# Scores and exp by halves of the queries, in the last two blocks of a cross-attention loop

## The chip, the cores and the metric

The kernel runs on one core of one Trainium2 chip. The metric is the device time in microseconds (us) of one execution. The engines are TensorE (PE in the profile; its weight loads are PEld), VectorE (DVE), ScalarE (ACT), GpSimd (POOL) and SyncE (SP), which issues most transfers.

## The reference

One block of a Perceiver: cross-attention of 512 tokens to a context of 8192, then linear attention, then a quantized feed-forward layer. The change touches the cross-attention only:

```python
x = x + xattn(layernorm(x), ctx, ctx, Wq, bq, Wk, bk, Wv, bv, Wo, bo)
# xattn, 16 heads of 32, x (1, 512, 512), ctx (1, 8192, 512), all f32:
q = split_heads(query @ Wq + bq)
k = split_heads(key @ Wk + bk)
v = split_heads(value @ Wv + bv)
scores = einsum('bhqd,bhkd->bhqk', q, k) / sqrt(d)
weights = softmax(scores, axis=-1)
z = einsum('bhqk,bhkd->bhqd', weights, v)
return merge_heads(z) @ Wo + bo
```

## The kernel before

The context is cut into 16 blocks of 512 positions. A block has 16 units: four groups `g` of four heads (32 rows each, so a group fills 128 partitions) times four chunks `k` of 128 context positions. The loop (line 837) runs over the 256 units in order of block, group, chunk. For a unit:

- `weights` (line 773) makes the scores: 8 matmuls, one for each head `j` and each half `h` of the 128 positions, that each write 64 partitions by 512 queries. Each shows as two instructions, so a unit has 16 (line 788). They go to `sc`, a PSUM tile of 128 x 4 x 512 f32: for each partition four rows of 512, one a head. The pool `ps_s` has one such tile. One ACT instruction then takes the exp of all 2048 columns into `ex` (line 797), a tile in SBUF with four buffers.
- Next on PE come steps from a queue of projections for later blocks (`ahead`; matmuls of line 388 into `pm` or `pk`, evicted by lines 405, 478, 481, 491), and the weighted sums of the *previous* unit (`weighted_sums`, line 733, into `av`). In the last block the weighted sums come first, then one step, and at times row sums of the exps (`sums`, line 751, into `dn`).
- DVE adds `ex` to a running sum `acc` (line 806), from which the softmax denominators come, and the finished `av` to `Z` (line 745).

How many projection steps a unit takes is planned by cost and due time: up to block 13 each block's work makes the next block's keys and values. In block 14 (total - 2) there is less, because part of the last block's keys (22 units of cost) is kept for the last block itself. Block 15 (total - 1) runs those, one step a unit, until they are used up.

All these instructions are kept in the order in which the program issues them on each engine; the framework adds the waits between engines.

After the loop follow the output projection (line 898), linear attention (lines 936 to 1123; `feat` of lines 1051 and 1073 are its features, with exps of 128 x 1024 at line 1029) and the feed-forward layer. The kernel has a second, exact variant (`exact`), taken only if a denominator is out of bounds; the change leaves it as it is.

Of the kernel before, what the change touches and what calls it, by code (L numbers as in the profile page):

```python
# [8 lines left out]
F32 = mybir.dt.float32  # L9
BF16 = mybir.dt.bfloat16  # L10
AF = mybir.ActivationFunctionType
# [5 lines left out]
P = 128  # L17
# [9 lines left out]
def network(  # L27
# [24 lines left out]
    nc = tc.nc  # L52
    S, E = x.shape
    L = ctxT.shape[1]
    FF = W1T.shape[1]
    H, D = 16, 32
# [3 lines left out]
    HG = P // D  # L60
# [3 lines left out]
    SCALE = 1.0 / float(D) ** 0.5  # L64
# [12 lines left out]
    def in_order(i):  # L77

        return tc.keep_in_program_order(i)
# [6 lines left out]
    for i in range(7):  # L86
        n = 1 << i
# [190 lines left out]
    ap4 = ctx.enter_context(tc.tile_pool(name="ap4", bufs=4))  # L278
    ps_m = ctx.enter_context(tc.tile_pool(name="ps_m", bufs=2, space=PSUM))

    with ExitStack() as actx:
        aw = actx.enter_context(tc.tile_pool(name="aw", bufs=1))

        qT = aw.tile([P, NE, S], F32, name="qT")
# [11 lines left out]
        bias = aw.tile([P, NE], F32, name="bias")  # L296
# [4 lines left out]
        ct, kT, vt, tt = {}, {}, {}, {}  # L301
# [4 lines left out]
        total = first + NB  # L306
# [418 lines left out]
        ps_s = sctx.enter_context(tc.tile_pool(name="ps_s", bufs=1, space=PSUM))  # L725
# [36 lines left out]
        def biased(g):  # L762
# [5 lines left out]
            else:  # L768
                in_order(nc.vector.tensor_scalar(
                    Z[:, g, :], Z[:, g, :], bv_sb[:, g : g + 1], None, ALU.add  # L770
                ))

        def weights(b, g, k):

            assert ("k", b, g, k // 2) in made
            sc = ps_s.tile([P, HG, S], F32, name="sc")
            if exact:
                for j in range(HG):
                    for h in range(2):
                        in_order(nc.tensor.matmul(  # L780
                            sc[ts(h, P // 2), j, :], lhsT=ones_h[ds(j * D, 3), ts(h, P // 2)],
                            rhs=mrow[ds(j * D, 3), g, :], start=True, stop=False,
                        ))

            for j in range(HG):
                rows = ts(j, D)
                for h in range(2):
                    in_order(nc.tensor.matmul(  # L788
                        sc[ts(h, P // 2), j, :],
                        lhsT=kT[b][rows, g, ds(k * P + h * P // 2, P // 2)],  # L790
                        rhs=qT[rows, g, :], start=not exact, stop=True,
                    ))
            ex = ap4.tile([P, HG, S], F32, name="ex")
            if exact:
                in_order(nc.scalar.activation(ex, sc, AF.Exp, scale=SCALE))
            else:
                in_order(nc.scalar.activation(  # L797
                    ex, sc, AF.Exp, bias=bias[:, g : g + 1], scale=SCALE
                ))
            return ex  # L800
# [35 lines left out]

        for i, u in enumerate(units):
            ex = weights(*u)
            if i >= last_block:
                b, g, k = u  # L840
# [470 lines left out]
    for q in range(NF // 4):  # L1311
# [14 lines left out]
        for i in range(4):  # L1326
# [8 lines left out]
            if f < 2 or i % 2 == 1:  # L1335
                k = f if f < 2 else f // 2 + 1
# [33 lines left out]
    for i in range(len(chunks) + 1):  # L1370
        if i < len(chunks):
            f, n = chunks[i]
# [4 lines left out]
        f, n = chunks[i - 1]  # L1377
# [18 lines left out]
@with_exitstack  # L1396
def perceiver_block(ctx: ExitStack, tc: tile.TileContext, **args):
    nc = tc.nc
    fate = ctx.enter_context(tc.tile_pool(name="fate", bufs=1))
    wrong = fate.tile([1, 1], mybir.dt.int32, name="wrong")  # L1400
    network(tc, False, wrong, **args)
    again = nc.values_load(wrong, min_val=0, max_val=1)
    with tc.If(again > 0):
        network(tc, True, None, **args)
# [50 lines left out]
```

## Time and profile before

| what | value |
|---|---|
| median of 3 runs | 1117.11 us (1117.04 to 1119.11) |
| the profiled execution | 1118.67 us, span 1116.9 us |
| granted TensorE clock, mean | 0.995 |
| block 14 (848.7 to 902.2): PE, DVE, ACT busy | 51.34, 43.67, 32.54 us of 53.50 |
| block 15 (902.2 to 955.8): PE, DVE, ACT busy | 49.10, 43.88, 34.52 us of 53.60 |
| granted clock in both | 1.00 |

Times in the profile are counted from the start of the span. A line of the timeline has the start, the duration, engine, source line, operation, output and inputs, shapes and count; the brackets give how long the engine was idle before it and whose end released it. Several instructions of one kind in a row are merged, and the duration is then that of the whole row. Matmuls are pipelined and their ends are modelled, so a start is surer than an end. A line of a group has, behind the bar, busy us, mean ns of one, and idle us before them. A line of the waits has total us, times, and the longest. A line of a stretch has its length, then busy us (and instructions) of PE, PEld, DVE, ACT and POOL, then the granted clock and what the transfers took.

### The profile page before, as it was taken

How to read it: one execution, taken by the hardware profiler on the slowest of the kernel's cores; microseconds unless marked ns; L12 is line 12 of the kernel's file. 1: busy time of each engine (PE TensorE's matmuls, PEld its weight loads, DVE VectorE, ACT ScalarE, POOL GpSimd, SP SyncE). 2: the span in 40 equal slices, each digit the busy share in tenths (PEclk: the TensorE clock that was granted, in tenths of full speed). 3: DMA queues.
4: the chain of work that ended last, by engine and by line, in shares of the span. 5: the costliest groups of instructions: out<-in, count | busy, mean ns of one | idle time of the engine just before them, and what ended most of it. 6: DMA issues, size and time to landing. Idle time of an engine off the chain costs nothing.

```text
span 1116.9 us, 31051 instructions
## 1 busy us (share of the span) xinstructions
PE 1089.1 (98%) x14331; PEld 409.7 (37%) x14336; DVE 932.2 (83%) x863; ACT 633.7 (57%) x425; POOL 177.8 (16%) x90
## 2 busy tenths in 40 slices
PE   8999999999999999999999999999999999999896
PEld 5433333333333333333333333333332321344342
DVE  3688999999888888888888888888888888756796
ACT  2155555566666666666665555555555566346253
POOL 3520303011403030403030303030300000023000
PEclk9999999999999999999999999999999999999999
DMA  7121213110302121212010101010110021130001
GB/s 264 38 79 40 96 40 96 58 59 30 95 31 68 50 76 30 75 51 68 30 58 2 40 2 40 2 39 2 40 39 2 2 77 39 38 151 2 1 1 41
DMA packets 24778, 55.56 MB, mean 50 GB/s; under 512 B 1984, under 2 KB 2496, under 8 KB 24384
## 3 DMA queue, kind: packets, MB, share of 16 engines
q1 hardware_dynamic: 24352, 52.97, 14.3%
q8 instruction: 114, 1.87, 0.7%
q10 hardware_dynamic: 288, 0.52, 0.1%
q14 instruction: 24, 0.20, 0.1%
HBM read 48.25 MB, written 5.24 MB: 48 GB/s over the span
## 4 chain that ended last, share of the span: by engine, by line
PE 88%; ACT 5%; DVE 5%; issue 1%; DMA 1%; SPq 0%; DVEq 0%; ACTq 0%
PE pm L388 35%; PE sc L788 24%; PE av L733 18%; ACT ex L797 4%; PE po L898 2%; PE pq L1007 2%; PE pq L136 1%; DVE unchanged L143 1%; PE pv L936 1%; PE pys L1356 1%; DVE de L1122 1%; ACT er L1029 1%; PE att L1112 1%; DMA ct<-in_ctxT 1%; DVE tops L631 0%
## 5 line engine op out<-in xcount | busy, mean ns | idle before, releaser
L797 ACT ACTIVATE ex<-sc,bias 128x2048 f32<-128x2048 f32 x256 | 504.3, 1970 | 358.4 <-PE sc L788 358.4
L806 DVE TENSOR_TENSOR acc<-acc,ex 128x2048 f32<-128x2048 f32 x248 | 584.8, 2358 | 73.2 <-ACT ex L797 72.9
L788 PE MATMUL sc<-qT,kT 32*64 32x512 f32 x4096 | 285.2, 613 | 6.9 <-ACT ex L797 6.7
L733 PE MATMUL av<-ex,vt 128*32 128x512 f32 x2048 | 266.9, 593 | 0.0
L383 POOL TENSOR_TENSOR tt<-ct 128x512 f32<-128x512 f32 x32 | 62.4, 1950 | 573.4 <-DMA ct<-in_ctxT 519.8
L788 PEld LDWEIGHTS sc<-qT,kT 32*64 32x64 f32 x4096 | 59.7, 129 | 221.8 <-ACT ex L797 198.0
L388 PE MATMUL pm<-w,tt 128*32 128x256 f32 x2048 | 127.0, 382 | 0.0
L388 PE MATMUL pm<-tt,w 128*32 128x256 f32 x1920 | 118.0, 382 | 0.0
L388 PE MATMUL pm<-w,ct 128*32 128x256 f32 x1536 | 96.5, 383 | 0.0
L478 DVE TENSOR_TENSOR vt<-vt,pm 128x512 f32<-128x512 f32 x112 | 75.3, 684 | 25.1 <-PE pm L388 24.1
L388 PEld LDWEIGHTS pm<-w,tt 128*32 128x32 f32 x2048 | 59.7, 109 | 86.0 <-issue 51.9
L388 PE MATMUL pm<-ct,w 128*32 128x256 f32 x1440 | 90.1, 383 | 1.2 <-DMA ct<-in_ctxT 1.2
L733 PEld LDWEIGHTS av<-ex,vt 128*32 128x32 f32 x2048 | 65.3, 110 | 55.5 <-issue 14.0
L383 POOL TENSOR_TENSOR tt<-ct,tt 128x512 f32<-128x512 f32 x32 | 85.3, 2666 | 1.3
L388 PEld LDWEIGHTS pm<-tt,w 128*32 128x32 f32 x1920 | 56.5, 109 | 77.6 <-issue 46.2
L388 PEld LDWEIGHTS pm<-w,ct 128*32 128x32 f32 x1536 | 43.3, 109 | 73.8 <-issue 47.0
L388 PEld LDWEIGHTS pm<-ct,w 128*32 128x32 f32 x1440 | 41.2, 109 | 67.2 <-issue 44.1
L478 DVE TENSOR_TENSOR kT<-kT,pm 128x512 f32<-128x512 f32 x60 | 40.8, 680 | 27.6 <-PE pm L388 27.0
L481 DVE SCALAR_TENSOR_TENSOR kT<-pm,bk_sb,kT 128x256 f32<-128x256 f32 x90 | 39.0, 474 | 2.9 <-PE pm L388 1.0
L745 DVE TENSOR_TENSOR Z<-Z,av 128x512 f32<-128x512 f32 x60 | 40.6, 677 | 0.0
L1029 ACT ACTIVATE er<-feat 128x1024 f32<-128x1024 f32 x32 | 30.2, 1029 | 9.7 <-PE feat L1051 7.4
L1033 DVE SCALAR_TENSOR_TENSOR f<-er 128x1024 f32<-128x1024 f32 x16 | 19.9, 1248 | 13.6 <-ACT er L1029 13.6
(181 smaller groups left out, 585.7 us busy)
## 6 DMA issues: line engine op xcount, KB each, us to landing
ct<-in_ctxT SPq DMA_DIRECT2D x15, 1024.0 KB, 5.3
wraw<-in_W1T SPq DMA_DIRECT2D x16, 512.0 KB, 3.8
wraw<-in_W2T SPq DMA_DIRECT2D x16, 512.0 KB, 3.8
wd<-wquant SPq DMA_DIRECT2D x16, 256.0 KB, 2.4
w_q<-wd SPq DMA_DIRECT2D x2, 2048.0 KB, 10.6
w<-in_w_qkv SPq DMA_DIRECT2D x3, 1024.0 KB, 5.1
w<-in_Wk SPq DMA_DIRECT2D x2, 512.0 KB, 6.5
ct<-in_ctxT SPq DMA_DIRECT2D x2, 512.0 KB, 7.5
```

The source lines that it names most:

```text
L383: in_order(nc.gpsimd.tensor_tensor(tt[b][:, i], x, y, ALU.subtract))
L388: in_order(nc.tensor.matmul(ps[ts(j, D)], lhsT=lhsT[:, ts(j, D)], rhs=rhs, start=start, stop=stop))
L478: in_order(nc.vector.tensor_tensor(dst, src, ps, ALU.add))
L481: in_order(nc.vector.scalar_tensor_tensor(dst[:, m, :], ps[:, m, :], bk_sb[:, 2 * i + m : 2 * i + m + 1], src[:, m, :], ALU.add, ALU.add,))
L733: in_order(nc.tensor.matmul(av[g][ts(j, D), :], lhsT=vt[b][:, k, ds(g * P + j * D, D)], rhs=ex[:, j, :], start=(k == 0), stop=(k == NC - 1),))
L745: in_order(nc.vector.tensor_tensor(Z[:, g, :], Z[:, g, :], ps, ALU.add))
L788: in_order(nc.tensor.matmul(sc[ts(h, P // 2), j, :], lhsT=kT[b][rows, g, ds(k * P + h * P // 2, P // 2)], rhs=qT[rows, g, :], start=not ex ...
L797: in_order(nc.scalar.activation(ex, sc, AF.Exp, bias=bias[:, g : g + 1], scale=SCALE))
L806: in_order(nc.vector.tensor_tensor(acc[:, g], acc[:, g], ex, ALU.add))
L898: in_order(nc.tensor.matmul(po, lhsT=lhsT[:, c, ts(t, P)], rhs=w[:, c, :], start=(c == 0), stop=(c == NE - 1),))
L1007: in_order(nc.tensor.matmul(ps, lhsT=wt[:, c, ts(g, P)], rhs=ynT[:, c, :], start=(c == 0), stop=(c == NE - 1),))
L1029: in_order(nc.scalar.activation(er[-1][:, d].rearrange("p a n -> p (a n)"), ps[h], function))
```

## The change

In blocks 14 and 15, `weights` makes the scores of queries 0 to 255 for all heads, takes their exp, then makes the scores of queries 256 to 511 and takes theirs. The matmuls are twice as many with 256 columns each, and so are the exps with 1024 columns (four runs of 256). The tile `sc` is allocated once, in the first of these units, and kept for all 32 of them. The order of everything else stays.

```diff
+        halved = {}
+
         def weights(b, g, k):
 
             assert ("k", b, g, k // 2) in made
+            if not exact and b >= total - 2:
+
+
+                if "sc" not in halved:
+                    halved["sc"] = ps_s.tile([P, HG, S], F32, name="sc")
+                sc = halved["sc"]
+                ex = ap4.tile([P, HG, S], F32, name="ex")
+                for q in range(2):
+                    n = ts(q, S // 2)
+                    for j in range(HG):
+                        rows = ts(j, D)
+                        for h in range(2):
+                            in_order(nc.tensor.matmul(
+                                sc[ts(h, P // 2), j, n],
+                                lhsT=kT[b][rows, g, ds(k * P + h * P // 2, P // 2)],
+                                rhs=qT[rows, g, n], start=True, stop=True,
+                            ))
+                    in_order(nc.scalar.activation(
+                        ex[:, :, n], sc[:, :, n], AF.Exp, bias=bias[:, g : g + 1], scale=SCALE
+                    ))
+                return ex
             sc = ps_s.tile([P, HG, S], F32, name="sc")
```

## The prediction

> **What bounds the kernel now.** I read the page first (busy shares, the chain that ended last), then the groups of instructions by shape, then the timeline of the last two blocks, 848.73 to 955.77 us, and who waited there.
>
> ```profile
> PE 1089.1 (98%) x14331; PEld 409.7 (37%) x14336; DVE 932.2 (83%) x863; ACT 633.7 (57%) x425; POOL 177.8 (16%) x90
> ...
> PE 88%; ACT 5%; DVE 5%; issue 1%; DMA 1%; SPq 0%; DVEq 0%; ACTq 0%
> ```
>
> TensorE (PE) carries the chain. Its busy time is modelled, so I take the spacing of starts instead, in one unit of the last block (timeline; start, duration):
>
> ```profile
> 905.46 0.24 PEld L788 LDWEIGHTS sc<-qT,kT 32*64 32x64 f32 x16 [1.18 <-ACT ex L797]
> 905.46 1.12 PE L788 MATMUL sc<-qT,kT 32*64 32x512 f32 x16 [0.28 <-ACT ex L797]
> ...
> 906.51 1.07 PE L733 MATMUL av<-ex,vt 128*32 128x512 f32 x8
> 906.68 1.97 ACT L797 ACTIVATE ex<-sc,bias 128x2048 f32<-128x2048 f32 x1 [1.27 <-PE sc L788]
> ...
> 907.39 1.04 PE L388 MATMUL pk<-ct,w 128*32 128x512 f32 x8
> ...
> 908.70 0.69 PE L788 MATMUL sc<-qT,kT 32*64 32x512 f32 x8 [0.27 <-ACT ex L797]
> ```
>
> A unit is scores (16 matmul instructions, 1.05 us to the next start), then weighted sums and projections, while ScalarE (ACT) does the exp. The exp starts 1.22 after the scores, takes 1.97, and the next scores start 0.04 later: 3.24 in all. The rest of PE's work would have been done sooner. How much sooner, the weight loads say: before scores that don't wait they are idle for 0.84, before those that do for 1.18, so the wait is 0.34.
>
> ```profile
> 879.14 0.23 PEld L788 LDWEIGHTS sc<-qT,kT 32*64 32x64 f32 x16 [0.84 <-ACT ex L797]
> ```
>
> The waits of 848.7 to 955.8:
>
> ```profile
> PEld sc L788 <- ACT ex L797: 34.6, 32, 2.0
> ...
> PE sc L788 <- ACT ex L797: 6.4, 20, 1.1
> ...
> PE dn L751 <- ACT ex L797: 0.3, 1, 0.3
> ```
>
> So 21 of the 32 units wait for an exp: 18 for 0.34, two for 0.40 and one, at 942.22, for 1.20 (2.04 less 0.84). That is 6.1 + 0.8 + 1.2 = 8.1 us, all that there is to win here. The other 11 are bound by PE's work alone (3.33 to 3.76 each).
>
> **What the change does to a unit.** It issues the same columns in twice the instructions: scores of queries 0 to 255 for all four heads (S0), their exp (E0), scores of 256 to 511 (S1), their exp (E1). Everything turns on one question: may PE write S1 while ACT still reads E0's half, and the next S0 while ACT reads E1's? Both halves lie in the same four 512-column rows of `sc`, one row a head; E0 reads all four rows and each S1 matmul writes one of them. Nothing in this trace shows it: every PSUM tile of the kernel before is written whole before it is read. The nearest row is an early eviction by halves (timeline):
>
> ```profile
> 12.65 1.93 PE L388 MATMUL pm<-ct,w 128*32 128x256 f32 x32
> ...
> 14.74 0.48 DVE L481 SCALAR_TENSOR_TENSOR kT<-pm,bk_sb,kT 128x256 f32<-128x256 f32 x1 [1.02 <-issue]
> ```
>
> These 32 matmuls fill columns 0 to 255 of one 512-column row first and 256 to 511 with the last 16. The VectorE (DVE) addition reads only the first half, ready at about 13.7; DVE was idle from 13.72, yet it starts at 14.74, behind the end of all 32 (14.58). The profile names no releaser, so this is a strong hint, not proof, that the program orders accesses by whole rows. I take "held": S1 waits for E0, and the next S0 for E1. The other bound, "free", is priced below.
>
> The Trainium skill speaks against the change here: PSUM — Partial Sum Buffer, section "PSUM bank collisions raise a hardware error", says that TensorE must not write a 2 KiB bank of PSUM, in the same 32 partitions, while ScalarE reads it, even at disjoint columns, and that the program's semaphores have to keep them apart. By that rule a row of 512 f32 is one such bank and only "held" can run, at the sum below; without it "free" would stay open, at 1109 us. No run here shows a collision.
>
> **The cost of a held unit.** Rows for the half exp and for short scores:
>
> ```profile
> L797 ACT ACTIVATE ex<-sc,bias 128x2048 f32<-128x2048 f32 x256 | 504.3, 1970 | 358.4 <-PE sc L788 358.4
> ...
> L1029 ACT ACTIVATE er<-feat 128x1024 f32<-128x1024 f32 x32 | 30.2, 1029 | 9.7 <-PE feat L1051 7.4 <-PE feat L1073 2.3
> L236 ACT ACTIVATE wquant<-wraw,neg_magic 128x1024 bf16<-128x1024 f32 x16 | 18.2, 1136 | 0.0
> ...
> 987.04 1.21 PE L1051 MATMUL feat<-proj_sb,kT 32*64 32x128 f32 x64
> 988.17 3.27 PE L1007 MATMUL pq<-ynT,w 128*128 128x512 f32 x7
> 988.28 2.85 ACT L1029 ACTIVATE er<-feat 128x1024 f32<-128x1024 f32 x3 [0.55 <-PE feat L1051]
> ```
>
> - Half exp: 1.03 (an exp of 128x1024 without a bias column, half of them strided just like this one) to 1.14 (with a bias column, out of SBUF). Between L797 and the 0.69 of a 128x512 activation with bias (L1117) a straight line gives 1.115; I take that. It also makes 2.23 of ACT time a unit in place of 1.97, which is hidden: ACT is idle for 40 of these 107 us.
> - Half scores: 64 instructions of 128 columns pass in 1.13 (987.04 to 988.17), 16 of 512 in 1.05: the same columns, so 16 of 256 cost 0.52 to 0.565. I take 0.52. The doubled weight loads (0.13 each, overlapping) cost nothing extra in L1051's row; if they showed, 0.565 prices them.
> - From the last scores' pace to the exp: 1.22 - 1.05 = 0.17 at 512 columns, 0.11 at 128 (988.28 - 988.17). I take 0.14.
>
> S0's start to S1's start: 0.52 + 0.14 + 1.115 + 0.045 = 1.82. S1 then runs 0.52 and the other work follows as before. So PE's unit is its old work plus 1.82 + 0.52 - 1.05 = 1.29: E0 has no work behind which to hide, because weighted sums and projections are queued behind S1 on PE. E1 is hidden: 0.14 + 1.115 + 0.045 = 1.30 after S1, beside 1.85 of sums and projections. The old waits for the exp vanish. One unit (938.98, with no projection left) has only about 0.97 there and stays bound by ACT, at 2 x 1.82 = 3.64 instead of 3.33 (3.24 - 1.20 + 1.29).
>
> Sum over the 32 units: 32 x 1.29 = 41.3, less 8.1 of old waits, plus 0.3: 33.5. Five evictions by ACT (four L405 of 0.68, one L491) end about 0.2 after the next S0 is ready to be read, so they delay E0: +1.0. DVE loses nothing: it is busy 87.6 of 107.1 and its units get longer. No transfer is late: the last weights of this stretch are issued by 939 and first read at 972. Total +34.5: the span goes from 1116.9 to 1151.4, the profiled execution from 1118.67 to 1153.2; the median of the runs lies 1.56 below that execution, so 1117.11 becomes 1151.6.
>
> The Trainium skill's ScalarE: Activation LUTs, "What ACT_TABLE_LOAD costs", gives 280 ns + 0.833 ns an element with a bias column, that is 1.133 for a half; the sum by it, an estimate, would be 0.6 us more than by my 1.115.
>
> **Rivals.**
> 1. Free (faster). If the program lets PE write one half of a row while ACT reads the other, exps and scores overlap, and PE never waits: the 8.1 us come back, less about 0.2 where the unit without projection is bound by two exps: 1109.2. It decides if S1 starts before E0 ends. For it: ACT and PE each have room, and DVE just fits (35.2 busy in the 40.0 us from 902.2 to 942.2, which would shrink to 35.7). Against: the eviction at 14.74. Chance 0.05.
> 2. Held, and PE's clock drops (much slower). PE would be idle for a third of each unit. Two stretches point either way (PE busy, then clock):
>
> ```profile
> 1037.00:1048.00 11.00, 8.98 (x47) 2.70 (x50) 6.70 (x5) 4.46 (x5) 0.00 (x0) 0.85 0.00 0
> ...
> 1090.00:1100.00 10.00, 6.64 (x29) 2.52 (x29) 8.37 (x24) 4.80 (x6) 0.00 (x0) 1.00 0.00 1
> ```
>
> At 0.85 the 2.9 us of PE's work in a unit grow by 0.51, 16 us in all: 1168. The gaps here are short (1.3) and come every 4 us, so I give 0.05.
> 3. It changes nothing: the halves run, but each unit's PE work hides E0 as well. That needs sums or projections ahead of S1, and the code issues them after it: 1117. Chance 0.01.
>
> **How the numbers follow.** Held at full clock has 0.89. Its own bounds: half exp 1.03 to 1.14 gives -2.7 to +0.8 (32 units, once each on PE's path), the pace up to 0.565 in both halves +2.9, the latency 0.11 to 0.17 plus or minus 1.0, the delayed E0 -1.0 to +1.0. Together some 1147 to 1157; I widen by 1 for terms that I have not seen: 1146 to 1158, about 0.82 of the chance. A measurement of this kernel can tell 0.2% (2.2 us): slower 0.94 (held, with either clock), same 0.01, faster 0.05.
>
> **What would show it.** Right: 64 half exps near 1.115; in each unit PE idle for about 1.2 before S1, released by the half exp; S1 starting 0.04 after E0 ends; 71 us for block 14 and 70 for block 15, in place of 53.5 each; nothing moved after the loop. Wrong: S1 rows that start during E0 (free), a clock under 1.00 in the loop's end (rival 2), or a half exp whose time is not half of the columns.

## The result, and the profile after

The changed kernel takes 1159.8 us (median of 4 runs, 1159.4 to 1160.5) against 1118.0 for the kernel before beside it: a ratio of 1.0371, 95% interval 1.0358 to 1.0385. That is 41.8 us slower, where 34.5 were forecast: the direction was right and S1 is held as forecast, but the size was too small, and the time lies 1.8 us above the range. The profiled execution took 1159.36, its span 1157.4.

The groups of shapes in the stretch of the last two blocks (848 to 1000 us):

```profile
L795 ACT ACTIVATE ex<-sc,bias 128x1024 f32<-128x1024 f32 x64 | 71.3, 1113 | 70.6 <-PE sc L790 70.6
...
L790 PE MATMUL sc<-qT,kT 32*64 32x256 f32 x1024 | 44.1, 399 | 41.3 <-ACT ex L795 41.3
```

The 64 half exps take 1.113 us each, and PE is idle for 41.3 us before scores, waiting for one (6.4 before the change, in these 32 units). One unit on the timeline, with the next:

```profile
864.40 0.69 PE L790 MATMUL sc<-qT,kT 32*64 32x256 f32 x16
865.20 1.11 ACT L795 ACTIVATE ex<-sc,bias 128x1024 f32<-128x1024 f32 x1 [2.22 <-PE sc L790]
...
866.37 0.69 PE L790 MATMUL sc<-qT,kT 32*64 32x256 f32 x16 [1.27 <-ACT ex L795]
...
866.99 1.06 PE L388 MATMUL pk<-ct,w 128*32 128x512 f32 x8
867.16 1.11 ACT L795 ACTIVATE ex<-sc,bias 128x1024 f32<-128x1024 f32 x1 [0.85 <-PE sc L790]
...
868.84 0.69 PE L790 MATMUL sc<-qT,kT 32*64 32x256 f32 x16
```

S1 starts 0.06 after the end of E0 (865.20 + 1.11): it is held. From S0 to S1 it is 1.97, forecast 1.82. From S1 to the next work it is 0.62, forecast 0.52. Behind that come sums and projections as before, and E1 is hidden beside them. PE's clock is 1.00 through the whole stretch (first numbers after the length: busy us of PE, PEld, DVE, ACT):

```profile
849.36:924.00 74.64, 54.26 (x936) 19.65 (x936) 44.01 (x29) 36.69 (x34) 0.00 (x0) 1.00 0.05 16
924.00:996.00 72.00, 51.11 (x776) 14.30 (x768) 43.84 (x23) 37.70 (x36) 0.00 (x0) 1.00 0.09 30
```

From the first scores of block 14 to the last row sums (997.92) it is 148.56 us, against 107.04 before: 41.5 more. The remainder cancels in part: 0.6 more ahead of block 14 and 1.65 less after the loop, in one execution of each; neither was studied.

### The profile page after: what moved, and what is told of

Same layout as the page of the kernel before. It is cut to its first block, busy times and chain, and to the rows that moved or that the text cites. A ratio compares the mean times of both kernels' runs of the same rounds, so it can differ in the third digit from the quotient of the medians.

```text
span 1157.4 us, 32114 instructions
## 1 busy us (share of the span) xinstructions
PE 1095.7 (95%) x14848; PEld 417.7 (36%) x14848; DVE 932.5 (81%) x863; ACT 642.1 (55%) x457; POOL 176.5 (15%) x90
## 4 chain that ended last, share of the span: by engine, by line
PE 89%; DVE 4%; ACT 4%; issue 1%; DMA 1%; SPq 0%; ACTq 0%; DVEq 0%
PE pm L388 35%; PE sc L811 20%; PE av L733 19%; PE sc L790 4%; ACT ex L795 3%; PE pq L1030 2%; PE po L921 2%; PE pk L388 1%; PE pq L136 1%; DVE unchanged L143 1%; PE pv L959 1%; PE pys L1379 1%; DVE de L1145 1%; ACT er L1052 1%; PE dn L751 1%
## 5 line engine op out<-in xcount | busy, mean ns | idle before, releaser
L820 ACT ACTIVATE ex<-sc,bias 128x2048 f32<-128x2048 f32 x224 | 441.2, 1970 | 318.5 <-PE sc L811 318.5
L811 PE MATMUL sc<-qT,kT 32*64 32x512 f32 x3584 | 249.5, 613 | 0.5 <-ACT ex L820 0.3
L383 POOL TENSOR_TENSOR tt<-ct 128x512 f32<-128x512 f32 x32 | 57.2, 1789 | 574.8 <-DMA ct<-in_ctxT 520.4
L811 PEld LDWEIGHTS sc<-qT,kT 32*64 32x64 f32 x3584 | 52.1, 129 | 187.2 <-ACT ex L820 163.4
L795 ACT ACTIVATE ex<-sc,bias 128x1024 f32<-128x1024 f32 x64 | 71.3, 1113 | 70.6 <-PE sc L790 70.6
L388 PEld LDWEIGHTS pm<-w,tt 128*32 128x32 f32 x2048 | 59.7, 109 | 83.5 <-issue 49.3
L383 POOL TENSOR_TENSOR tt<-ct,tt 128x512 f32<-128x512 f32 x32 | 89.2, 2786 | 1.3
L790 PE MATMUL sc<-qT,kT 32*64 32x256 f32 x1024 | 44.1, 399 | 41.3 <-ACT ex L795 41.3
L790 PEld LDWEIGHTS sc<-qT,kT 32*64 32x64 f32 x1024 | 15.0, 129 | 82.7 <-ACT ex L795 71.8
```

The lines of the kernel that those rows point to most:

```text
L383: in_order(nc.gpsimd.tensor_tensor(tt[b][:, i], x, y, ALU.subtract))
L388: in_order(nc.tensor.matmul(ps[ts(j, D)], lhsT=lhsT[:, ts(j, D)], rhs=rhs, start=start, stop=stop))
L790: in_order(nc.tensor.matmul(sc[ts(h, P // 2), j, n], lhsT=kT[b][rows, g, ds(k * P + h * P // 2, P // 2)], rhs=qT[rows, g, n], start=True, ...
L795: in_order(nc.scalar.activation(ex[:, :, n], sc[:, :, n], AF.Exp, bias=bias[:, g : g + 1], scale=SCALE))
L811: in_order(nc.tensor.matmul(sc[ts(h, P // 2), j, :], lhsT=kT[b][rows, g, ds(k * P + h * P // 2, P // 2)], rhs=qT[rows, g, :], start=not ex ...
L820: in_order(nc.scalar.activation(ex, sc, AF.Exp, bias=bias[:, g : g + 1], scale=SCALE))
```

## The experiments

My theory: S1 is *held* until E0 ends, and since no other work is queued ahead of S1, PE stands still. Most of the loss is that wait (PE idles for 41.3 in place of 6.4 us, by its modelled ends), and the forecast was short because a short row of scores costs more than its columns. The rivals: the doubled number of instructions costs time in itself; the clock drops; and, on why it is held, rows of the tile or the tile as a whole.

**1. What do 256-column scores cost by themselves?** All 32 matmul instructions of a unit in one go, one exp:

```diff
                 for q in range(2):
                     n = ts(q, S // 2)
                     for j in range(HG):
...
-                    in_order(nc.scalar.activation(
-                        ex[:, :, n], sc[:, :, n], AF.Exp, bias=bias[:, g : g + 1], scale=SCALE
-                    ))
+                in_order(nc.scalar.activation(
+                    ex, sc, AF.Exp, bias=bias[:, g : g + 1], scale=SCALE
+                ))
```

> The scores in 256-column halves as in the change, all 32 matmul instructions in one go, then one exp of 2048 columns as before. Measures the price of the short matmuls without any wait between them. Account 'per burst' (a row of scores costs its columns, 0.43 for each 256, plus a fixed 0.19 to whatever follows and 0.37 to the exp, however many instructions it has): scores to next work stays at 1.05, scores to exp at 1.22, time as before, 1118 us within 1. Account 'per instruction' (the 0.62 that 16 instructions of 256 columns took in the changed kernel is 39 ns for each of them): 32 take 1.24, so 0.19 more in every unit, 32 x 0.19 = 6: 1124 us. The prediction's own 0.52 for 16 (columns alone): 1.05, as before, but then the 0.62 has no reason.

Measured: 1119.1 against 1119.2, ratio 0.9995 (0.9983 to 1.0007): no difference. Timeline of this kernel:

```profile
849.03 1.12 PE L790 MATMUL sc<-qT,kT 32*64 32x256 f32 x32
...
850.08 1.93 PE L388 MATMUL pm<-w,ct 128*32 128x256 f32 x32
850.26 1.97 ACT L795 ACTIVATE ex<-sc,bias 128x2048 f32<-128x2048 f32 x1 [1.37 <-PE sc L790]
```

32 short instructions take 1.05 to the next work and 1.23 to the exp, just like 16 long ones. So twice the instructions are free, and 16 short ones, at 0.62, are not half of 1.05. Two points give the account: 0.43 for the columns of a half, and 0.19 once for each row of scores, however long.

**2. Does that account hold at a quarter?**

```diff
-                for q in range(2):
-                    n = ts(q, S // 2)
+                for q in range(4):
+                    n = ts(q, S // 4)
```

> Four quarters of 128 queries in place of two halves. Account 'per burst' (0.21 for the columns of a quarter, 0.37 to the exp, 0.69 for an exp of 512 columns as in the row of line 568, 0.045 back): 1.32 from quarter to quarter, three times, then 0.21 + 0.19: 4.35 in place of 1.05, 3.30 more in each unit, 32 x 3.30 - 8.1 = 97: 1215 us. By the prediction's numbers (columns alone, 0.26 a quarter, 0.14 to the exp): 1.13 from quarter to quarter, 2.61 more in each unit, 32 x 2.61 - 8.1 = 75: 1193 us.

Measured: 1285.6 (a single run), 166 more than before, where neither account gave more than 97. The first unit, at a clock of 1.00, is what the account "per burst" says (timeline):

```profile
851.09 0.47 PE L790 MATMUL sc<-qT,kT 32*64 32x128 f32 x16
...
852.41 0.48 PE L790 MATMUL sc<-qT,kT 32*64 32x128 f32 x16 [0.85 <-ACT ex L795]
...
855.06 0.48 PE L790 MATMUL sc<-qT,kT 32*64 32x128 f32 x16 [0.84 <-ACT ex L795]
...
855.47 3.08 PE L388 MATMUL pm<-w,ct 128*32 128x256 f32 x32
```

It is 1.32 from quarter to quarter, and 0.41 from the last quarter to the next work (0.21 + 0.19; columns alone would be 0.26). Then the clock falls, and with it goes the sum (stretches; the clock is the number behind the five busy times):

```profile
865.00:880.00 15.00, 11.12 (x136) 3.10 (x128) 4.58 (x2) 4.19 (x7) 0.00 (x0) 0.61 0.00 0
880.00:910.00 30.00, 21.26 (x328) 7.76 (x335) 9.85 (x5) 11.19 (x17) 0.00 (x0) 0.67 0.01 2
```

So the total decides nothing here, the spacing at full clock does. And the second rival of the prediction is a real mechanism: it did not act in the profiled run of the change, but in the one run of the next step in the same direction it did.

**3. Is the loss the time beside E0?** The previous unit's weighted sums are put right behind E0's issue, ahead of S1 (the loop's own calls of them, further down, become `between()`):

```diff
+                    if q == 0:
+                        between()
                 return ex
...
-            ex = weights(*u)
+            before, adds = [], []
+
+            def between():
+                while late:
+                    before.append(late[0][-1])
+                    adds.append(weighted_sums(*late.pop(0)))
+
+            ex = weights(*u, between)
...
```

> The change, with the weighted sums of the previous unit put between the two halves on TensorE, right behind the issue of the first exp, so that 0.88 of work lies beside the first exp. Theory (the loss is TensorE's idle time beside the first exp, since no work is queued ahead of the second scores): the wait before the second scores falls by 0.88 or so, and a unit is then bound by ScalarE's chain of two held halves, 2 x 1.96 = 3.92, where 2.9 to 3.3 was TensorE's work; 4.4 in the three units with row sums. Block 14 about 63, block 15 about 64, together 127 in place of 107: 1138 us (1135 to 1142). Rival (the loss is in the twice as many instructions themselves, not in the wait): nothing comes back, 1159.

Measured: 1140.8 against 1119.2, ratio 1.0188 (1.0167 to 1.0210): 21.6 slower, so about half of the loss is back, within the expected range. Timeline:

```profile
857.38 0.69 PE L790 MATMUL sc<-qT,kT 32*64 32x256 f32 x16 [0.28 <-ACT ex L795]
...
859.34 0.69 PE L790 MATMUL sc<-qT,kT 32*64 32x256 f32 x16 [0.28 <-ACT ex L795]
...
859.96 1.06 PE L733 MATMUL av<-ex,vt 128*32 128x512 f32 x8
...
861.30 0.69 PE L790 MATMUL sc<-qT,kT 32*64 32x256 f32 x16 [0.28 <-ACT ex L795]
```

PE's idle time before S1 fell from 1.27 to 0.28, and scores now start every 1.96: the chain of two held halves sets the pace, 3.92 for a unit where a whole one took 3.24. Instructions are as many as in the change, so their number is not the cause.

**4. Why is it held: rows?** The halves by heads, in rows of their own, in the same kept tile:

```diff
                 for q in range(2):
-                    n = ts(q, S // 2)
-                    for j in range(HG):
+                    two = ts(q, HG // 2)
+                    for j in range(2 * q, 2 * q + 2):
...
-                        ex[:, :, n], sc[:, :, n], AF.Exp, bias=bias[:, g : g + 1], scale=SCALE
+                        ex[:, two, :], sc[:, two, :], AF.Exp, bias=bias[:, g : g + 1], scale=SCALE
```

(the matmuls write `sc[..., j, :]` from `qT[rows, g, :]`, all 512 queries).

> The same split into two scores and two exps in the last two blocks, but by heads: scores and exp of heads 0 and 1, then of 2 and 3, all 512 queries, in the same tile that is kept. The order of the score matmuls is then that of the kernel before. Theory 'rows' (in the change the second scores wait for the first exp because both halves lie in the same four 512-column rows of the scores' tile): the two halves now lie in different rows, so nothing is held; TensorE never waits for an exp in these units, the first exp starts before the end of all scores, and up to the 8.1 us of old waits come back: 1110 us (1109 to 1113). Theory 'tile' (the wait comes from writing a tile that ScalarE is reading, wherever): the second scores are held as well, 8 matmul instructions on half of the array take 0.85, so start to start 0.85 + 0.37 + 1.11 + 0.05 = 2.38, a unit grows by 2.38, and 32 x 2.38 - 8.1 = 68: 1186 us.

Measured: 1225.9, ratio 1.0962 (1.0936 to 1.0989). Held, although no matmul of S1 writes a row that E0 reads (timeline, and one stretch):

```profile
869.48 1.09 PE L790 MATMUL sc<-qT,kT 32*64 32x512 f32 x8
870.63 1.11 ACT L795 ACTIVATE ex<-sc,bias 128x1024 f32<-128x1024 f32 x1 [3.76 <-PE sc L790]
...
871.80 1.09 PE L790 MATMUL sc<-qT,kT 32*64 32x512 f32 x8 [1.24 <-ACT ex L795]
...
872.82 1.07 PE L388 MATMUL pk<-ct,w 128*32 128x512 f32 x8
```

```profile
970.00:1000.00 30.00, 25.03 (x144) 4.85 (x143) 14.00 (x8) 10.71 (x10) 0.00 (x0) 0.73 0.00 1
```

S1 starts 0.06 after the end of E0 (870.63 + 1.11). The theory "rows" falls. S0 to S1 is 2.32, expected 2.38 by "tile"; the excess over 1186 comes with a clock of 0.73 to 0.89 in these stretches.

**5. Or the tile?** The same by heads, in two tiles of two rows each:

```diff
-                if "sc" not in halved:
-                    halved["sc"] = ps_s.tile([P, HG, S], F32, name="sc")
-                sc = halved["sc"]
+                if not halved:
+                    sctx.close()
+                    ps_h = sctx.enter_context(tc.tile_pool(name="ps_h", bufs=1, space=PSUM))
+                    for q in range(2):
+                        halved[q] = ps_h.tile([P, HG // 2, S], F32, name=f"sc{q}")
...
```

(the tiles come from a pool opened anew; matmuls and exps use `halved[q]`).

> By heads as in the run by heads before it, which was held although its halves lay in different rows, but with the scores of heads 0 and 1 and those of heads 2 and 3 in two tiles of their own (two rows each), kept for the 32 units. Same instructions, same order. Theory 'tile' (the program waits by whole tiles: a matmul that writes a tile waits for the last instruction that reads it, wherever in the tile): now nothing is held inside a unit, scores run as one row of 1.05, the first exp starts before the second scores end, TensorE never waits for an exp and its clock stays at 1.00. Up to 8.1 us less than before: 1111 us against 1119 (1110 to 1115). Rival (the wait is not the tile's but comes with two exps and two scores on the two engines, for instance because the second scores have to follow the first exp in whatever order is kept between them): 1226 as by heads.

Measured: 1117.3 against 1118.8, ratio 0.9985 (0.9976 to 0.9994). The wait inside the unit is gone, 108 us against the run by heads, by nothing but the two tiles (timeline):

```profile
904.10 1.11 PE L792 MATMUL sc<-qT,kT 32*64 32x512 f32 x16
...
905.26 2.12 ACT L797 ACTIVATE ex<-sc,bias 128x1024 f32<-128x1024 f32 x2 [1.21 <-PE sc L792]
...
907.00 1.51 PE L792 MATMUL sc<-qT,kT 32*64 32x512 f32 x16
...
907.43 0.21 PEld L792 LDWEIGHTS sc<-qT,kT 32*64 32x64 f32 x8 [0.22 <-ACT ex L797]
...
910.30 1.11 PE L792 MATMUL sc<-qT,kT 32*64 32x512 f32 x16
```

So in one tile the second scores wait because the program orders these accesses by whole tiles. But I expected 1111, and that was wrong. The first exp starts 1.16 after the scores, not at half time: two heads are finished hardly sooner than all four (1.22), as if all of them ran side by side on the array (in number 4 two heads alone took 1.15). Both exps then end at 907.38, after 907.00, where PE is ready for the next scores; the second eight of those wait until 907.43, and run alone. A pair of units takes 6.20 in place of 6.48, and only part of the old wait comes back.

**6. Two tiles in all 256 units** (the condition without `b >= total - 2`).

> Two tiles by heads in all 256 units. In the first 14 blocks TensorE's work alone is longer than the chain through the exp (only about a quarter of a microsecond of wait in all of the page's idle time of the scores' matmuls outside the last two blocks), so theory 'tile' gives the same time as with two tiles in the last two blocks, 1111 (1109 to 1115); ScalarE has 0.26 us more in each unit, which is hidden behind its 1.4 of idle time. Rival: evictions by ScalarE and the exps get into each other's way there, or the hold is back: slower than the former by more than 3 us.

Measured: 1116.1 against 1118.8, ratio 0.9978 (0.9968 to 0.9988): the fastest version here, by 2.7 us. It is not told apart from number 5, whose interval overlaps; the level of 1111 failed for the same reason.

**7. The second exp alone.** Scores whole, as in the kernel before, then two half exps (the cut is against number 1):

```diff
-                in_order(nc.scalar.activation(
-                    ex, sc, AF.Exp, bias=bias[:, g : g + 1], scale=SCALE
-                ))
+                for q in range(2):
+                    n = ts(q, S // 2)
+                    in_order(nc.scalar.activation(
+                        ex[:, :, n], sc[:, :, n], AF.Exp, bias=bias[:, g : g + 1], scale=SCALE
+                    ))
```

> Scores whole as before (16 matmul instructions of 512 columns), then two exps of 256 queries each, one behind the other, in the last two blocks. Measures what the second exp alone costs. From the rows: scores to exp 1.22, two exps of 1.113 that overlap by about 0.1, 0.045 back: 3.39 for the chain in place of 3.24. Units that waited take 0.15 more, those of 3.33 take 0.06 more: about 18 x 0.15 + 8 x 0.06 = 3.2 us over the kernel before. If the exps do not overlap: 3.49, about 6 us.

Measured: 1122.7 against 1118.8, ratio 1.0040 (1.0027 to 1.0053), 3.9 us where 3.2 were expected. Waiting units go from 3.24 to 3.40 (907.34 to 910.73 in its timeline, 3.39): two exps in a row cost 2.12.

**8. The change in block 15 alone** (the condition with `total - 1`).

> The change in the last block only. By the sum with the sizes that the changed kernel showed (1.96 + 0.62 - 1.05 = 1.53 for each unit, less the old waits of that block, 5.4, plus 0.35 for the unit without a projection): 16 x 1.53 - 5.4 + 0.35 = 19.4 over the kernel before, and the clock at 1.00. If the loss came from a drop of the clock or from something that builds up over the two blocks, it would be far from half of the 41.

Measured: 1141.0 (2 runs), ratio 1.0197 (1.0179 to 1.0216), 20 to 24 us where 19.4 were expected. That is about half of the 41, so nothing builds up over the two blocks. In the profiled execution (1140.25) block 15, from its first scores (904.14) to the last row sums (979.01), takes 21.3 more than before (902.22 to 955.77). Of these, 1.7 lie in one place: from the S1 at 960.73 to the next scores at 964.89 it is 4.16, where the same step of the changed kernel (981.33 to 983.80) takes 2.47. The row sums in it took 1.90 in place of 1.06, at a clock of 0.56 from 961.0 to 964.6. That leaves 19.6, close to the sum.

## Why the prediction was right and wrong, point by point

**The 8.1 us to win, in 21 waiting units**: not tried by itself. With the wait gone (number 5) PE's rows show no idle time before scores, but part of it has turned into the slower second half of a row of scores.

**Held: right, but not for my reason.** I read the addition at 14.74 us as ordering by 512-column rows. It fits ordering by tiles as well, and number 4 against 5 shows that it is the tile. Both readings hold this change, so there was luck in it: for the halves by heads mine would have been wrong. The Trainium skill (PSUM — Partial Sum Buffer, "PSUM bank collisions raise a hardware error") forbids halves in one bank to overlap, and so agrees with the change being held; but by its rule the halves by heads need not have been held, and they were: 1226 us. Whether halves in one row could ever overlap here was not tried.

**The step that failed: the cost of a half row of scores.** I took 0.52 because 64 instructions of 128 columns and 16 of 512 need about the same time; but both rows hold the same number of columns, so they could show only that more instructions cost nothing, never what *fewer columns* cost. The halves are two short rows of scores, each followed by a wait or by matmuls of another tile shape, and each has its fixed part. From S1 to the next work it measured 0.62, outside my bounds of 0.52 to 0.565. From S0 to its exp it measured 0.80, where I had 0.52 + 0.14 = 0.66. Together that is 0.24 more in a unit, 7.7 us in 32. The trace of before had the fixed part in plain sight: `av` to `pk`, two kinds of work of one shape, follow each other every 0.88, and scores, of another shape, take 1.05.

**The sum with the measured sizes.** 1.97 + 0.62 - 1.05 = 1.54 for each of 32 units is 49.3; less 8.1, plus 0.35 for the unit bound by ACT: 41.5, as measured in that stretch. The half exp (1.113, forecast 1.115) and the work that hides E1 were right. The 1.0 us for ACT's evictions was not there: such an eviction starts at 868.17 and ends within the 0.80 that the next half exp has to wait anyway. In all 32 units the first exp starts 0.79 to 0.86 after its scores.

**The clock**: right for this change. It was 1.00 in the stretch, and the mean of a whole run was 0.994 to 0.996 in its four runs, against 0.994 to 1.000 for the kernel before. But the forecast was near the edge: numbers 2 and 4 show it at 0.61 to 0.89, and number 8 lost 1.7 us to it in units like these.

**Nothing moved after the loop**: right within 1.65 us.

## What to carry to other kernels

Splitting a producer and a consumer in two lets them overlap in this kernel only if the parts lie in different tiles; in one tile they took turns, and in-order work queued behind the second part stood still meanwhile. Before splitting, ask what is queued between the two parts on the waiting engine. And price a shorter piece from rows that differ in total length, not from rows of equal length cut into more instructions: only the first show the fixed part, which is then paid once a piece.

## What the runs showed of the hardware that I had not expected

- Leaving scores of 32x64 tiles for other work costs a fixed 0.19 us, and the exp starts 0.37 beyond the columns, at 128, 256 and 512 columns alike (by heads, on half of the tiles, 512 columns took 1.02 and 1.15 in place of 1.05 and 1.22). The Trainium skill, TensorEngine Tiling (Array Packing), "Key Properties", says that a change of the tiling mode drains TensorE; the 0.19 fits that, but no run here changes the mode alone, so the cause is argued, not shown.
- PE's clock depends on more than the share of time in which the profile calls it busy. The change left PE busy for 72% (107 of 148.5 us) at 1.00. By heads, with scores on half of the tiles at a time, PE was busy for 73% (5.80 of 8.00) from 849 to 857, also at 1.00, and then the clock was 0.50 from 858 to 861. The longest wait before scores was about 1.3 us in both. Four quarters waited for 1.0 us at most, but were busy for only 44% (1.96 of 4.50) from 851 to 855.5 at 1.00, ahead of the fall. The means of 0.73 to 0.89 by heads mix two levels: 0.50 as above, and 1.00 again from 868 to 874. What sets the limit stays open.
